# The gated layer's first state: 32x32 transposes on VectorE and a block exchange through DRAM, in place of TensorE transposes

## Chip, cores, metric

One core of one Trainium2 chip. The metric is the device time of one launch in microseconds (us), median over runs. All runs in this document were of the fast state. Runs sent together share one chip and the runs of the kernel before on it; other groups of runs were on other chips, so across groups I compare ratios to the kernel before.

## The reference, cut to what matters

Three graph-attention layers are followed by a gated graph layer, over 128 graphs of 128 nodes and 256 features, all f32:

```python
# --- layer 3 (adj_preln) ---
h = jnp.maximum(_layernorm(x, axis=-1), 0.0)     # the gated layer's first state
x = x + _L3_gnn_ref(h, adj, ...)

def _L3_gnn_ref(x, adj, weight, w_ih, w_hh, b_ih, b_hh):
    h = x
    for i in range(3):
        m = jnp.einsum('bnd,de->bne', h, weight[i])
        aggr = jnp.einsum('bst,bsd->btd', A, m)
        h = _gru_cell(aggr, h, w_ih, w_hh, b_ih, b_hh)
    return h
```

## The kernel before

Graphs go in 32 groups of four (T = 4 x 128 = 512 columns). `gat(g)` does the attention layers and ends with the normalised first state; `gru(g)` does three gated steps. The state is needed twice: node-major as `hn` (for the aggregation) and feature-major as `hT` (for the gates).

```python
def turned(v, pool, tag, name):                       # used in all four layers
    hT = pool.tile([P, KD, T], FT, tag=tag, name=f"hT_{name}")
    for k in range(KD):
        ps = bank("gat", f"hTp_{name}_{k}")
        for b in range(G):
            nc.tensor.transpose(ps[:, b * P : (b + 1) * P], v[:, b, k * P : (k + 1) * P], ident)
        if k % 2 == 0:
            nc.scalar.copy(hT[:, k, :], ps)
        else:
            nc.vector.tensor_copy(hT[:, k, :], ps)
    return hT

# the tail of gat(g)
nm, rs = stats(xt, f"{g}_3")
nc.vector.tensor_mul(nm, nm, rs)
hn = grp.tile([P, G, D], FT, tag="hn0", name=f"hn_{g}_0")
for b in range(G):
    nc.scalar.activation(hn[:, b, :], xt[:, b, :], AF.Relu, bias=nm[:, b : b + 1], scale=rs[:, b : b + 1])
hT = turned(hn, grp, "h0", f"{g}_3")
# ... cut ...

# gru(g), one step: matmuls named nn, r, z read the state h; r, ni, z read the aggregate ag
def evac(k):                                          # steps 1 and 2: node-major state
    if i > 0:
        ps = node_major(i, k)                         # hnp: TensorE transposes into the one "tr" bank
        t = rw.tile([P, G, P], FT, tag=f"hn{k}", name=f"hn_{name}_{k}")
        nc.scalar.copy(t.rearrange("p b d -> p (b d)"), ps)
# ... cut ...
def aggregate(k):                                     # agp: into the same "tr" bank
    ps = bank("tr", f"agp_{name}_{k}")
    for b in range(G):
        nc.tensor.matmul(ps[:, b * P : (b + 1) * P], hn[k][b], am[:, b, :], start=True, stop=True)
    t = rw.tile([P, T], FT, tag=f"ag{k}", name=f"ag_{name}_{k}")
    nc.vector.tensor_copy(t, ps)
    ag.append(t)
# ... cut ...
AHEAD = 2
for g in range(min(AHEAD, NG)):
    run(gat(g))
for g in range(NG):
    run(gru(g))
    if g + AHEAD < NG:
        run(gat(g + AHEAD))
```

The program is emitted in that order, and a scheduler gives each engine a fixed order from it ahead of time (in the trace the 344 matmuls of a turn come in one order for 20 turns). The engines run their orders in parallel (the busy shares of 97%, 57% and 42% below overlap in one span). In the trace the attention of one group runs beside the gated steps of the group before it.

## Time and profile before

| | before |
|---|---|
| time, median | 3158.55 us |
| busy: TensorE / VectorE / ScalarE | 97% / 57% / 42% |
| one turn of a group in the steady part | 95.53 us, 30 of them nearly alike |
| TensorE transposes of the first state | 256 of 128x128, 8 a group |
| output stores: first at | 214.26 us |

In a row of the groups by line or of the timeline, PE is TensorE's matmuls, PEld its weight loads, DVE VectorE, ACT ScalarE. The names are output<-inputs. Brackets or the last column give the idle time just before, and what ended it. For example, in the waits of PE:

```profile
PE hnp L312 <- DVE ag L342: 37.5, 30, 1.5
```

This says that TensorE stood idle 37.5 us in 30 places, once a group and 1.5 us at the longest, before the node-major transposes, until DVE had copied the aggregate out of the bank that both share. A bank is one of the PSUM tiles (`bank(...)` in the code) that TensorE writes its results to.

### The profile page before, as it was taken

To read this page: it belongs to the slowest core of one execution; us is meant where nothing else is said; L and a number is where in the kernel's file an instruction comes from. 1 tells how busy PE (TensorE), PEld (TensorE's weight loads), DVE (VectorE), ACT (ScalarE), POOL (GpSimd) and SP (SyncE) were. 2 spreads that over 40 slices of the span, in tenths; PEclk is the share of its full clock that TensorE was granted. 3 is DMA by queue.
4 is the path that set the end of the run, shared out by engine and by line. 5 is a ranking of instruction groups with operands and counts; after the bars stand their busy time and mean duration, and the time that the engine had idled before them with its cause. 6 is when DMAs were issued, how large, how long until landed. Compare 5 with 4: busy or idle time off the path is not lost.

```text
span 3155.9 us, 31261 instructions
## 1 busy us (share of the span) xinstructions
PE 3049.1 (97%) x11093; PEld 1730.8 (55%) x11093; DVE 1785.9 (57%) x3960; ACT 1316.4 (42%) x2881; POOL 262.3 (8%) x358
## 2 busy tenths in 40 slices
PE   5799999999999999999999999999999999999999
PEld 3455555555555555555555555555555555555554
DVE  4555565555655555655555655556555555555553
ACT  1344444444444444444444444444444444444442
POOL 0110100010101001100001100101000001010000
PEclk8899999999999999999999999999999999999999
DMA  2000000000000000000000000000000000000000
GB/s 84 11 17 17 11 7 17 17 17 13 15 7 17 17 17 10 14 11 17 17 17 11 7 17 17 17 17 10 7 17 17 17 11 17 7 14 7 7 1 14
DMA packets 56188, 47.94 MB, mean 15 GB/s; under 512 B 3296, under 2 KB 55648, under 8 KB 56032
## 3 DMA queue, kind: packets, MB, share of 16 engines
q1 hardware_dynamic: 56032, 45.95, 4.6%
q8 instruction: 87, 1.43, 0.2%
q14 instruction: 69, 0.57, 0.1%
HBM read 29.17 MB, written 16.78 MB: 15 GB/s over the span
## 4 chain that ended last, share of the span: by engine, by line
PE 79%; DVE 11%; ACT 6%; issue 3%; DMA 1%; POOL 0%; SPq 0%; ACTq 0%; DVEq 0%; POOLq 0%
PE r L321 18%; PE z L321 16%; PE whp L207 10%; PE nn L321 9%; PE ni L321 8%; PE agp L338 4%; PE hTp L183 4%; PE hp L256 4%; DVE st L167 3%; DVE u L264 3%; DVE xo L268 2%; PE hnp L312 2%; PE atp L248 2%; ACT pe L232 2%; PE e L216 1%
## 5 line engine op out<-in xcount | busy, mean ns | idle before, releaser
L321 PE MATMUL r<-ag,wc 128*128 128x512 f32 x768 | 381.3, 597 | 0.0
L321 PE MATMUL ni<-ag,wc 128*128 128x512 f32 x768 | 371.3, 592 | 0.0
L321 PE MATMUL z<-ag,wc 128*128 128x512 f32 x768 | 366.0, 592 | 0.0
L207 PE MATMUL whp<-w,hT 128*128 128x258 f32 x1536 | 361.5, 385 | 0.7 <-ACT hT L187 0.7
L207 PEld LDWEIGHTS whp<-w,hT 128*128 128x128 f32 x1536 | 286.8, 191 | 90.5 <-ACT hT L187 39.1
L222 DVE SCALAR_TENSOR_TENSOR em<-e,wh,cap 128x128 f32<-128x128 f32 x384 | 108.1, 344 | 397.3 <-PE e L216 397.3
L367 ACT ACTIVATE r<-r,brz 128x512 f32<-128x512 f32 x192 | 131.9, 687 | 457.5 <-PE r L321 457.5
L211 ACT ACTIVATE wh<-whp,rs 128x258 f32<-128x258 f32 x384 | 183.0, 477 | 264.9 <-PE whp L207 264.7
L369 DVE SCALAR_TENSOR_TENSOR n<-r,wn 128x512 f32<-128x512 f32 x192 | 130.7, 681 | 263.5 <-ACT r L367 263.5
L362 ACT ACTIVATE wn<-nn,bh 128x512 f32<-128x512 f32 x192 | 131.3, 684 | 326.4 <-PE nn L321 326.4
L321 PE MATMUL nn<-h,whh 128*128 128x512 f32 x512 | 264.8, 599 | 0.0
L321 PE MATMUL z<-h,whh 128*128 128x512 f32 x512 | 263.2, 595 | 0.1
L321 PE MATMUL r<-h,whh 128*128 128x512 f32 x512 | 261.6, 592 | 0.0
L338 PEld LDWEIGHTS agp<-am,hn 128*128 128x128 f32 x1536 | 203.3, 193 | 64.4 <-issue 47.6
L321 PEld LDWEIGHTS z<-ag,wc 128*128 128x128 f32 x768 | 143.5, 190 | 168.0 <-issue 167.9
L374 ACT ACTIVATE n<-n,bi 128x512 f32<-128x512 f32 x192 | 137.8, 718 | 233.6 <-DVE n L373 233.6
L244 POOL TENSOR_SCALAR xm<-xo 128x1024 f32<-128x1024 f32 x64 | 66.9, 1045 | 1965.4 <-DVE xo L268 1965.4
L321 PEld LDWEIGHTS ni<-ag,wc 128*128 128x128 f32 x768 | 140.8, 190 | 153.0 <-issue 153.0
L262 ACT ACTIVATE t<-hp 128x512 f32<-128x512 f32 x192 | 114.6, 597 | 263.4 <-PE hp L256 263.3
L264 DVE SCALAR_TENSOR_TENSOR u<-hp,xm 128x512 f32<-128x512 f32 x192 | 132.0, 688 | 149.8 <-ACT t L262 149.8
L338 PE MATMUL agp<-am,hn 128*128 128x128 f32 x1536 | 208.0, 275 | 0.0
L342 DVE COPY ag<-agp 128x512 f32<-128x512 f32 x192 | 130.9, 682 | 124.2 <-PE agp L338 124.2
(84 smaller groups left out, 4400.4 us busy)
## 6 DMA issues: line engine op xcount, KB each, us to landing
x<-in_x_dram SPq DMA_DIRECT2D x32, 512.0 KB, 3.9
out_dram<-o SPq DMA_DIRECT2D x32, 512.0 KB, 2.9
adj<-in_adj_dram SPq DMA_DIRECT2D x32, 256.0 KB, 2.8
w<-in_L_gnn_W_dram SPq DMA_DIRECT2D x3, 256.0 KB, 6.4
ab<-in_L_gnn_a_dram SPq DMA_DIRECT2D x3, 256.0 KB, 6.2
whh_ld<-in_L_gnn_w_hh_dram SPq DMA_DIRECT2D x1, 768.0 KB, 8.2
wih_ld<-in_L_gnn_w_ih_dram SPq DMA_DIRECT2D x1, 768.0 KB, 6.1
gt_ld<-in_L_gnn_weight_dram SPq DMA_DIRECT2D x3, 256.0 KB, 3.6
```

Source lines behind the costliest of these rows:

```text
L183: nc.tensor.transpose(ps[:, b * P : (b + 1) * P], v[:, b, k * P : (k + 1) * P], ident)
L207: nc.tensor.matmul(ps[:, :E], hT[:, k, c * P : (c + 1) * P], W[l][:, k, :], start=(k == 0), stop=(k == KD - 1),)
L211: nc.scalar.activation(wh[:, c, :], ps[:, :E], AF.Copy, scale=rs[:, c : c + 1])
L256: nc.tensor.matmul(hp[:, b * D : (b + 1) * D], at[:, c * P : (c + 1) * P], wh[:, c, :D], start=True, stop=True,)
L264: nc.vector.scalar_tensor_tensor(u, hp, 0.0, xm[:, 2 * j : 2 * j + 2, :].rearrange("p b d -> p (b d)"), op0=OP.max, op1=OP.add,)
L321: nc.tensor.matmul(ps, w[:, k, c * P : (c + 1) * P], v[k], start=start, stop=stop)
L338: nc.tensor.matmul(ps[:, b * P : (b + 1) * P], hn[k][b], am[:, b, :], start=True, stop=True)
L342: nc.vector.tensor_copy(t, ps)
L362: nc.scalar.activation(wn, nn, AF.Identity, bias=bh[:, cn : cn + 1])
L367: nc.scalar.activation(r, pr, AF.Tanh, bias=brz[:, cr : cr + 1], scale=0.5)
L369: nc.vector.scalar_tensor_tensor(n, r, 1.0, wn, op0=OP.add, op1=OP.mult)
L374: nc.scalar.activation(n, n, AF.Tanh, bias=bi[:, cn : cn + 1])
```

## The change

The intent is to take 256 transposes off the busiest engine. VectorE transposes 32x32 blocks (in the trace of after, 64 instructions of 128x512 at 0.69 us) in place of TensorE's 128x128, and one write to DRAM with four reads puts the blocks where a full transpose has them. The five further runs that use this exchange gave the right result; no_transpose, which leaves the block transposes out, is off by a relative error of 0.18. The state then lies in runs of 32 columns, so the matmuls and the subtraction of step 0 read it through a pattern of three dimensions.

```diff
-        hT = turned(hn, grp, "h0", f"{g}_3")
+        tr = gw.tile([P, Q, KD, G, 32], FT, tag="hT", name=f"tr_{g}_3")
+        for k in range(KD):
+            nc.vector.transpose(
+                tr[:, :, k].rearrange("p j b c -> p b j c"),
+                hn[:, :, k * P : (k + 1) * P].rearrange("p b (j r) -> p b j r", j=Q),
+            )
+        d = dram.tile([Q, 32, Q, KD * G * 32], FT, tag="d", name=f"d_{g}")
+        nc.sync.dma_start(
+            d.rearrange("q r j f -> (q r) j f"), tr.rearrange("p j k b c -> p j (k b c)")
+        )
+        hT = grp.tile([P, Q, KD, G, 32], FT, tag="h0", name=f"h_{g}_0")
+        for j in range(Q):
+            nc.sync.dma_start(
+                hT[j * 32 : (j + 1) * 32].rearrange("p q k b c -> p q (k b c)"),
+                d[:, :, j, :].rearrange("q r f -> r q f"),
+            )
 # ... cut ...
-        h = [h0[:, k, :] for k in range(KD)]
+        h = [h0[:, :, k].rearrange("p q b c -> p b q c") for k in range(KD)]
 # ... cut: like(t, v) gives the other operand the same dimensions ...
-                    ps, w[:, k, c * P : (c + 1) * P], v[k], start=start, stop=stop
+                    like(ps, v[k]), w[:, k, c * P : (c + 1) * P], v[k], start=start, stop=stop
-                nc.vector.tensor_sub(d, h[c], n)
+                nc.vector.tensor_sub(like(d, h[c]), h[c], like(n, h[c]))
```

More of the change, by code (lines that the diff above doesn't have):

```diff
@@ L62 @@
     BANKS = {"gat": 3, "gru": 4, "tr": 1}
+    Q = P // 32
     def bank(tag, name):
@@ L158 @@
     setup.close()
+    dram = ctx.enter_context(tc.tile_pool(name="dram", bufs=2, space=bass.MemoryType.DRAM))
     rw = ctx.enter_context(tc.tile_pool(name="rw", bufs=2))
@@ L315, in node_major, with like @@
             return ps
+        def like(t, v):
+            return t.rearrange("p (b q c) -> p b q c", b=G, q=Q) if len(v.shape) == 4 else t
         for i in range(STEPS):
```

## The prediction

> **What bounds the kernel now.** I read the page first: its busy shares, its tenths by slice, and the groups by line.
>
> ```profile
> PE 3049.1 (97%) x11093; PEld 1730.8 (55%) x11093; DVE 1785.9 (57%) x3960; ACT 1316.4 (42%) x2881; POOL 262.3 (8%) x358
> PE   5799999999999999999999999999999999999999
> ```
>
> PE is busy in every slice but the first two, while DVE and ACT are near half. That alone would say that any PE work taken away comes off the time. The modelled ends of matmuls flatter PE, though, so I checked by starts. In the timeline two matmuls of 128x512 start every 0.86 us (0.43 us each, so some 0.107 us for 128 columns). Adding this over one turn of a group (start of one "hTp<-hn" batch to the next, 376.88 to 472.41 us) gives about 90.5 us of streaming in 95.53 us. The steady kernel repeats itself every 95.5 us, some 95% of it PE, the rest small gaps. The largest single gap is the 1.2 us at which the node-major transpose waits for the DVE copy of the aggregate (37.5 us over 30 times in the table of waits).
>
> Then the work that the change takes out, in the groups by line (line, engine, operation, out<-in, count, busy us and mean ns, idle before):
>
> ```profile
> L183 PE MATMUL hTp<-ident,hn 128*128 128x128 f32 x256 | 46.5, 286 | 11.9 <-ACT hn L294 7.6
> L187 ACT COPY hT<-hTp 128x512 f32<-128x512 f32 x128 | 74.9, 585 | 50.3 <-PE hTp L183 46.7
> L189 DVE COPY hT<-hTp 128x512 f32<-128x512 f32 x128 | 88.1, 688 | 104.3 <-PE hTp L183 104.3
> ```
>
> The first row is the disputed transposes alone: 256, that is 8 for each of 32 groups. The two copies serve all four layers, so a quarter (32 each) goes. What one group's batch costs is read in the timeline of PE in the steady part:
>
> ```profile
> 376.02 1.02 PE L321 MATMUL nn<-h,whh 128*128 128x512 f32 x2
> 376.88 0.96 PE L183 MATMUL hTp<-ident,hn 128*128 128x128 f32 x4
> 377.68 1.02 PE L321 MATMUL r<-h,whh 128*128 128x512 f32 x2
> 378.54 0.60 PE L183 MATMUL hTp<-ident,hn 128*128 128x128 f32 x4
> 378.98 1.02 PE L321 MATMUL z<-h,whh 128*128 128x512 f32 x2
> 379.84 1.05 PE L338 MATMUL agp<-am,hn 128*128 128x128 f32 x8
> ```
>
> By starts, the first four take 0.80 us (377.68 - 376.88; 0.37 us over streaming, as each waits for an ACT slice of hn) and the other four 0.44. One group: 1.24 us. The same pattern stands in groups 2 to 31.
>
> [...]The new moving operand of the step-0 matmuls comes in runs of 32 f32[...]; the trace of before has no such operand.
>
> **The change part by part**, for one group.
> PE loses 8 transposes: up to 1.24 us. ACT loses one copy of 0.585 us, DVE one of 0.688.
> DVE gains two transposes of 128x512. The tensor_tensor rows of that size take 0.684 to 0.692 us; I estimate 0.69 each, 1.38 for two. DVE net +0.69 us a group, 22 us in all: 57% busy becomes 58%, no bound.
> DMA: 512 KB written (the output's 512 KB landed in 2.9 us) and four reads of 128 KB (256 KB of adj landed in 2.8 us), with an issue of 0.37 us each on SP: an estimated 2 x 0.37 + 2.9 + 3 x 0.37 + 2.8 = 7.6 us, 9 with the DVE part. 32 MB more on queues that are 5% busy is nothing.
> Is that hidden? hn is complete at 378.2 us, and the first matmul on hT starts at 401.74: slack of 23 us, two and a half times what is needed. In steady groups, hidden. For group 0 it isn't: transposes at 112.49, first use at 115.92. There hn is ready at 113.9, h0 would come at about 123, 7 us later. PE has the next group's attention to do meanwhile, and saves 2 us of transposes; I charge +3 us. Group 1, where the transposes cost some 2.5 us (188.04 to 189.79, with a wait of 1.03), gives that back.
> Step-0 matmuls and the subtraction read the same elements in another order: 0.
>
> Does the 1.24 us come off? This is where I hesitate. What follows needs ACT and DVE, and both are dense just there:
>
> ```profile
> 376.15 2.08 ACT L294 ACTIVATE hn<-xo,nm,rs 128x256 f32<-128x256 f32 x4
> 378.13 0.67 ACT L379 ACTIVATE z<-z,brz 128x512 f32<-128x512 f32 x1
> 378.70 0.57 ACT L329 COPY hn<-hnp 128x512 f32<-128x512 f32 x1
> 379.17 0.58 ACT L187 COPY hT<-hTp 128x512 f32<-128x512 f32 x1
> ```
>
> The aggregate matmuls (agp, at 379.84) need the ACT copy that ends at 379.27, and that copy stands behind the four slices of hn. Without the transposes PE would be done with z at 378.98 + 0.86 - 1.24 = 378.60 and would wait for ACT until about 379.5 (end of the copy, plus some 0.2 us to the matmul, as now from copy to weight load and on). With this order of ACT the gain is 379.84 - 379.5 = 0.34 us, not 1.24. And the DVE copy that frees the single "tr" bank runs thus:
>
> ```profile
> 378.83 0.69 DVE L383 SCALAR_TENSOR_TENSOR d<-z,d 128x512 f32<-128x512 f32 x1 [0.51 <-ACT z L379]
> 379.44 0.68 DVE L189 COPY hT<-hTp 128x512 f32<-128x512 f32 x1
> 380.04 0.68 DVE L385 SCALAR_TENSOR_TENSOR h<-d,n 128x512 f32<-128x512 f32 x1
> 380.93 0.69 DVE L342 COPY ag<-agp 128x512 f32<-128x512 f32 x1 [0.21 <-PE agp L338]
> ```
>
> One DVE transpose fits nearly into the idle 0.51 us, the second takes the place of the copy. If both stand ahead of the ag copy, it starts at about 381.1 instead of the 380.6 that an earlier agp would allow, and the gain is gone.
>
> **The rivals**, for 30 steady groups, with start-up +0.5 (3 - 2.5).
> A: PE alone bounds, and the scheduler rearranges ACT so that nothing waits: 30 x 1.24 = 37 us, 3121. For it: 97% busy PE, near-zero gaps in the 20 us around. Against: the order of ACT above.
> B: the wait for hn transposed becomes a wait for the node-major copy on ACT: 30 x 0.34 = 10 us, 3148. For it: the timeline above, where that copy is 0.57 us ahead of its use.
> C: DVE delays the aggregate's copy by the second transpose: gain 0 to -0.1 us a group, 3158 to 3162. For it: DVE is 4.34 us busy of the 5.5 from 376.5 to 382.
> D: the step-0 matmuls (768, 24 a group) slow down on the runs of 32. A tenth more would be 768 x 0.043 = 33 us, and eat all of A.[...]
> E: the exchange isn't hidden and PE waits at each group's start: excluded by the slack of 23 us unless the transfers take three times my estimate.
> The instructions are ordered by a static scheduler, since attention of one group and recurrence of another are mingled in the trace though emitted apart. Removing instructions can shift that order everywhere, by some us either way; nothing in the profile sizes this.
>
> **Range and chances.** Weights: A 0.35, B 0.4, C 0.2, D or E 0.05 (taken at 3190). 0.35 x 3121 + 0.4 x 3148 + 0.2 x 3160 + 0.05 x 3190 = 3143; as schedules between A and B are likely when ACT loses a copy too, I move it to 3140, a gain of 0.6%. The range runs from just under A (3118) to the time before (3158). 2% is 63 us: more than all PE time of these transposes, so faster by 2% needs a lucky new order (0.02); slower by 2% needs D in force, or E (0.03).
>
> **What would show it.** Right: PE matmuls down by 256 and no "hTp<-hn" row; 64 DVE transposes near 0.69 us; step-0 matmuls still starting 0.43 us apart; the first matmul of a group on h0 not waiting for DMA, except in group 0; a turn of 94.3 us (A), 95.2 (B) or 95.5 (C) in place of 95.53. B shows as agp waiting for the ACT copy of hn, C as a longer wait of hnp for ag than 1.2 us a group. Wrong: DVE transposes well above 1 us, step-0 matmuls further apart, a DMA wait in front of nn, or a turn whose order of streams is altogether different.

## The result, and the profile after

The changed kernel takes 3143.81 us (3142.61 to 3145.15, 4 runs) against 3158.55. The ratio is 0.9952, with a 95% interval of 0.9935 to 0.9970. Ratios are the mean time of one kernel's fast runs over that of the other's in the same rounds, so not quite the ratio of the medians. The verdict by the 2% rule is "same", with a small gain clear of noise.

The page's busy line, and the row of the new operation in the groups by line:

```profile
PE 3017.8 (96%) x10837; PEld 1709.2 (54%) x10837; DVE 1803.2 (57%) x3992; ACT 1298.0 (41%) x2849; POOL 263.1 (8%) x358
L302 DVE STREAM_TRANSPOSE tr<-hn 128x512 f32<-128x512 f32 x64 | 41.7, 690 | 3.2 <-ACT hn L296 3.2
```

There are 256 matmuls fewer, and 64 block transposes of 0.69 us each (two in a row take 1.30). PE is still busy 96% of a shorter span. The same stretch of TensorE that the prediction showed now reads, in the timeline of PE:

```profile
380.25 1.02 PE L343 MATMUL nn<-h,whh 128*128 128x512 f32 x2
381.12 1.02 PE L343 MATMUL r<-h,whh 128*128 128x512 f32 x2
381.97 1.02 PE L343 MATMUL z<-h,whh 128*128 128x512 f32 x2
383.56 1.16 PE L360 MATMUL agp<-am,hn 128*128 128x128 f32 x8 [0.56 <-ACT hn L351]
384.55 0.82 PE L185 MATMUL hTp<-ident,xn 128*128 128x128 f32 x6
385.21 1.07 PE L343 MATMUL nn<-h,whh 128*128 128x512 f32 x2
386.11 0.60 PE L330 MATMUL hnp<-ident,h 128*128 128x128 f32 x4
```

The transposes are gone from between nn, r and z, and a wait stands where they were. The aggregate's matmuls come 1.59 us after the start of z, where z's streaming takes 0.86. The bracket names what TensorE waited for: the ACT copy of the node-major state. ACT at that time:

```profile
380.39 2.08 ACT L296 ACTIVATE hn<-xo,nm,rs 128x256 f32<-128x256 f32 x4
382.37 0.67 ACT L401 ACTIVATE z<-z,brz 128x512 f32<-128x512 f32 x1
382.94 0.57 ACT L351 COPY hn<-hnp 128x512 f32<-128x512 f32 x1
```

The order of ACT is the one of before, with the copy behind the four slices of hn; only the copy for hT behind it is gone. It ends at 383.51 and agp starts at 383.56. In the waits of PE over the whole run a row has appeared that wasn't there before:

```profile
PE agp L360 <- ACT hn L351: 16.9, 30, 0.6
```

To see the whole turn and not one place, I took every matmul's start from the trace, averaged over 20 steady groups. I called "streaming" the columns at 0.429 us for 512 (the median spacing within an unbroken run; the 258 columns of whp count as 256), and put the rest down as gaps in front of the instruction that came late. This ledger is my own sum from the traces, in us for one turn:

| | turn | streaming | gaps | before hTp<-hn | before agp | before hnp | before r<-ag |
|---|---|---|---|---|---|---|---|
| before | 95.58 | 90.95 | 4.64 | 0.39 | 0.22 | 1.51 | 0.22 |
| after | 94.91 | 90.09 | 4.82 | none | 1.06 | 1.51 | 0.41 |

The change takes 0.86 of streaming and 0.39 of gaps out, 1.25 in all, as the prediction sized it. Of that, 0.83 comes back before agp and 0.19 before r<-ag. Small gaps elsewhere fall by 0.45 together. The 0.19 is partly a trade with them: at one of the places where r<-ag now waits, the kernel before has a gap of 0.10 before a transpose of the attention (atp). The net is 0.67 us a turn, some 20 us over 30 turns. The first output store leaves at 219.16 us in place of 214.26, so the start costs 4.9 us. 20 less 5 is the 15 us measured.

### The profile page after: what moved, and what is told of

Read it like the earlier page. It is cut to its first block, busy times and chain, and to the rows that moved or that the text cites. A ratio compares the mean times of both kernels' runs of the same rounds, so it can differ in the third digit from the quotient of the medians.

```text
span 3141.2 us, 31050 instructions
## 1 busy us (share of the span) xinstructions
PE 3017.8 (96%) x10837; PEld 1709.2 (54%) x10837; DVE 1803.2 (57%) x3992; ACT 1298.0 (41%) x2849; POOL 263.1 (8%) x358
## 4 chain that ended last, share of the span: by engine, by line
PE 77%; DVE 11%; ACT 7%; issue 3%; DMA 1%; POOL 0%; SPq 0%; DVEq 0%; POOLq 0%; ACTq 0%
PE r L343 17%; PE z L343 15%; PE whp L209 11%; PE nn L343 9%; PE ni L343 8%; PE agp L360 5%; PE hp L258 4%; PE hTp L185 3%; DVE st L169 3%; DVE u L266 3%; DVE xo L270 2%; PE hnp L330 2%; ACT pe L234 2%; ACT hn L296 2%; PE atp L250 2%
## 5 line engine op out<-in xcount | busy, mean ns | idle before, releaser
L343 PE MATMUL nn<-h,whh 128*128 128x512 f32 x768 | 394.2, 595 | 1.6 <-DMA h<-d 1.2
L343 PE MATMUL r<-h,whh 128*128 128x512 f32 x768 | 393.2, 594 | 0.0
L343 PE MATMUL z<-h,whh 128*128 128x512 f32 x768 | 392.4, 592 | 0.0
L360 PE MATMUL agp<-am,hn 128*128 128x128 f32 x1536 | 212.9, 278 | 23.1 <-ACT hn L351 16.9
L343 PEld LDWEIGHTS r<-h,whh 128*128 128x128 f32 x768 | 141.0, 191 | 139.8 <-issue 117.2
```

Of the source, the lines that this page charges most:

```text
L343: nc.tensor.matmul(like(ps, v[k]), w[:, k, c * P : (c + 1) * P], v[k], start=start, stop=stop)
```

## The experiments

My theory at this point was that the ACT copy holds back what the transposes free (rival B of the prediction), against rival C, that DVE does. Nine kernels were run; each row is of one kernel and the last column its ratio to the kernel before.

| run | time, us | turn, us | ratio |
|---|---|---|---|
| after_tail_late | 3144.25 | 94.93 | 0.9951 |
| before_tail_late | 3142.58 | 95.05 | 0.9947 |
| after_hn_pool | 3342.11 | 101.29 | 1.0579 |
| no_transpose | 3150.44 | 95.12 | 0.9970 |
| after_tail_late_tr_behind | 3125.41 | 94.33 | 0.9891 |
| first_on_pe | 3140.79 | 94.93 | 0.9940 |
| best1 | 3122.86 | 94.38 | 0.9883 |
| layout_only | 3159.50 | 95.60 | 1.0000 |
| before_plus_exchange | 3157.13 | 95.49 | 0.9994 |

### after_tail_late and before_tail_late: only the order of ACT

The tail of `gat` is emitted inside the gated steps of the group before, behind its step-2 copies, so that the copy gets ahead of three of the four hn slices. The same edit is made to both kernels.

```diff
     for g in range(NG):
-        run(gru(g))
+        step = gru(g)
+        if g + 1 in tails:
+            advance(step, 13)          # past step 2's node-major copies and aggregates
+            run(tails.pop(g + 1))
+        run(step)
         if g + AHEAD < NG:
-            run(gat(g + AHEAD))
+            tails[g + AHEAD] = gat(g + AHEAD)
+            advance(tails[g + AHEAD], 12)   # all but the tail
```

> The changed kernel with one thing moved: the last part of a group's attention (statistics, scaled relu to hn, exchange) is emitted inside the recurrence of the group before, after its step-2 node-major copies, so that ACT does the node-major copy ahead of three of the four hn slices. Same instructions otherwise. Theory (the saved 1.24 us of PE turned into a wait of the aggregate for that ACT copy): the wait of agp for ACT hn, 16.9 us over 30 groups in the changed kernel, falls below 3 us, the turn of a group falls from 94.89 us to 94.3 to 94.5, the time to 3125 to 3133. Rival C (DVE's two transposes ahead of the ag copy bound): turn and time stay, 94.9 and 3144.

> The same move in the kernel before, as the control: is it the order alone that gains? Theory: with the transposes in place PE had only about 0.35 us to gain from an earlier copy, as PE reached agp just then, so a turn between 95.2 and 95.6 and 3148 to 3160. Rival (the new order alone gives the gain, whatever becomes of the transposes): a fall as large as between the changed kernel and its moved form, about 15 us, to 3143.

The theory failed in both, and in both the number of its rival came out. The wait for ACT did vanish, as wanted (gaps before agp 0.31 in place of 1.06), but the changed kernel stayed at 3144.25 us. The kernel before gained all of it: 3142.58, ratio 0.9947. With this order the change is worth nothing. PE and DVE of after_tail_late tell where the time went, in the timelines of the two engines:

```profile
385.01 1.05 PE L360 MATMUL agp<-am,hn 128*128 128x128 f32 x8
385.90 1.12 PE L343 MATMUL nn<-h,whh 128*128 128x512 f32 x2
386.86 1.02 PE L343 MATMUL r<-h,whh 128*128 128x512 f32 x2
388.25 0.66 PE L330 MATMUL hnp<-ident,h 128*128 128x128 f32 x4 [0.37 <-DVE ag L364]
```

```profile
385.76 0.16 DVE L172 TENSOR_SCALAR nm<-mv 128x4 f32<-128x4 f32 x1
386.32 1.30 DVE L302 STREAM_TRANSPOSE tr<-hn 128x512 f32<-128x512 f32 x2 [0.39 <-ACT hn L296]
387.55 0.65 DVE L364 COPY ag<-agp 128x512 f32<-128x512 f32 x1
390.78 0.69 DVE L364 COPY ag<-agp 128x512 f32<-128x512 f32 x1 [2.58 <-PE agp L360]
```

Now the hn slices come later, the two transposes wait for them at the head of DVE's order (0.39 us), and the copy of the aggregate stands behind. It starts at 387.55, 1.65 us after the aggregate's last matmul gave way to nn (385.90). TensorE needs that copy for the bank. The gap of the ledger before hnp grew from 1.51 to 2.09. So C stands behind B: take the wait for ACT away in this way and the wait for DVE takes its place. The edit has a part in that, as it delays three of the four hn slices that the DVE transposes need. The table of waits shows the second as hnp waiting 60 times (48.4 us) where the changed kernel waited 30.

The kernel before has no DVE transposes, so it can use the early copy. Its eight TensorE transposes now run as one batch once hn is complete, as the timeline of PE shows:

```profile
382.40 1.07 PE L338 MATMUL agp<-am,hn 128*128 128x128 f32 x8
383.31 1.04 PE L183 MATMUL hTp<-ident,hn 128*128 128x128 f32 x8
384.18 1.88 PE L321 MATMUL r<-ag,wc 128*128 128x512 f32 x4
```

The gap before them fell from 0.39 to 0.02, that before r<-ag from 0.22 to 0.03.

### after_tail_late_tr_behind: both waits out of the way

Kept from after_tail_late: the late tail. New: the DVE transposes are queued behind the first copy of the aggregate, where DVE was idle for 2.58 us.

```diff
+                cp = nc.vector.tensor_copy(t, ps)
+                if i == STEPS - 1 and k == 0:
+                    last_ag[g] = cp.ins
 # ...
+            with ExitStack() as behind:
+                if g - 1 in last_ag:
+                    behind.enter_context(tc.issue_after(last_ag[g - 1]))   # order only
+                nc.vector.transpose(...)
```

> The first run's theory fell as told: with the ACT copy early the wait for ACT is gone, but the turn stayed at 94.9 us, and the same move gained the kernel before 16 us. New theory: two waits lie one behind the other at this place. The changed kernel waits 0.73 us a group for the ACT copy; with that gone it waits for DVE, whose two transposes stand ahead of the copy of the aggregate (gaps of 0.54 us before hnp and 0.2 us within r<-ag). This run keeps the late tail and also queues the DVE transposes behind that copy, where DVE idled 2.6 us. Theory: the 0.54 and 0.2 go, turn 94.1 to 94.3, time 3118 to 3128. Rival (PE's streaming is not the floor here, something else of this schedule holds 94.9): turn and time stay within 0.1 us and 4 us of 94.93 and 3144.

It took 3125.41 us, ratio 0.9891, turn 94.33, as expected of the theory save 0.03 us on the turn. DVE's order is now the wanted one:

```profile
384.32 0.69 DVE L368 COPY ag<-agp 128x512 f32<-128x512 f32 x1 [0.17 <-PE agp L364]
384.93 1.29 DVE L306 STREAM_TRANSPOSE tr<-hn 128x512 f32<-128x512 f32 x2
388.39 0.69 DVE L368 COPY ag<-agp 128x512 f32<-128x512 f32 x1 [2.17 <-PE agp L364]
```

The gap before hnp fell from 2.09 to 1.54; that before r<-ag stayed at some 0.22, so the second part of the expectation (0.2 us there) was a miss. Against before_tail_late, the kernel that keeps its TensorE transposes in the same late order, the change is now worth 95.05 - 94.33 = 0.72 us a turn and, by the ratios, 0.56%. This pair shows most of the 0.86 of streaming arriving at last.

### no_transpose and before_plus_exchange: what the added parts cost

no_transpose (a wrong result on purpose) writes hn to DRAM as it is and reads it back by the same transfers.

```diff
-        tr = gw.tile(...)
-        for k in range(KD):
-            nc.vector.transpose(...)
# ... cut ...
-            d.rearrange("q r j f -> (q r) j f"), tr.rearrange("p j k b c -> p j (k b c)")
+            d.rearrange("q r j f -> (q r) j f"), hn.rearrange("p b (j f) -> p (b j) f", j=1)
```

> Wrong result on purpose: the changed kernel without its two DVE transposes, hn written to DRAM as it is and read back by the same five transfers. Tells what the DVE part costs. Theory (ACT copy bounds, DVE's 1.3 us lies beside it): turn 94.7 to 94.9, time 3139 to 3144. Rival C (the DVE part delays the aggregate's copy): turn down by 0.3 us or more, 3135 or less.

It took 3150.44 us, more than the changed kernel although it does less, so neither number held. The wait for the ACT copy is unchanged (gap of 0.73 us between z and agp in both). So is the gap before hnp, where a late copy of the aggregate would show (some 1.52 us a turn in both). With DVE's transposes absent neither the time nor these gaps fell, so in the changed kernel as it stands they are not what holds TensorE at this place. The 0.2 us a turn that this kernel loses comes with another static order: behind agp stands one attention transpose, where the changed kernel has six (the row at 384.55). The ledger finds nothing of the loss there. It lies in small gaps before matmuls of the attention (0.12 to 0.13 us more before each of hTp<-xn, atp and whp), less 0.19 before r<-ag. What makes them is not isolated.

before_plus_exchange adds the two DVE transposes, the write and the four reads to the kernel before, into a tile that nobody reads.

```diff
         hT = turned(hn, grp, "h0", f"{g}_3")
+        tr = ...; nc.vector.transpose(...)   # as in the change
+        d = ...;  hx = grp.tile(..., tag="hx", bufs=1)   # five transfers into hx
```

> The added parts alone: the kernel before still transposes on TensorE and uses that state; beside it each group also does the two DVE transposes, the write and the four reads into a tile that nobody reads. Theory (DVE's part stands ahead of the copy of the aggregate and has some 0.5 us too little room): the copy moves from 5.35 to about 5.9 us after the first nn of the step, the turn grows by 0.3 to 0.7 us, the time to 3168 to 3182. Rival (the added parts are hidden and cost nothing by themselves): 3156 to 3163.

It took 3157.13 us, ratio 0.9994 (0.9985 to 1.0003): the added parts cost nothing by themselves, as the rival said, and my theory was a miss. Its 5.35 us counts from the start of the node-major transposes (375.58 to 380.93), not from the first nn; by that count the copy now starts at 5.80. Again the order bent around them, as its timeline of PE shows:

```profile
382.00 1.05 PE L357 MATMUL agp<-am,hn 128*128 128x128 f32 x8
382.89 1.01 PE L186 MATMUL hTp<-ident,xn 128*128 128x128 f32 x6
383.74 1.07 PE L340 MATMUL nn<-h,whh 128*128 128x512 f32 x2
```

The copy is later, but six transposes of the next attention stand between agp and nn and TensorE works on them meanwhile. My theory had kept the old order of PE.

### after_hn_pool: hn on GpSimd

```diff
-            nc.scalar.activation(hn[:, b, :], xt[:, b, :], AF.Relu, bias=nm[...], scale=rs[...])
+            nc.gpsimd.tensor_scalar(hn[:, b, :], xt[:, b, :], rs[...], nm[...], op0=OP.mult, op1=OP.add)
+        nc.gpsimd.tensor_scalar(hn, hn, 0.0, None, op0=OP.max)
```

> The changed kernel with hn (the four scaled relu slices) computed on GpSimd in place of ACT, so ACT is free for the node-major copy. Theory: agp no longer waits for ACT, turn 94.3 to 94.6, time 3126 to 3135. Rival C (DVE): stays at 3144. A second way to be wrong: GpSimd is slower on these and hn comes late, which costs nothing as the exchange has over 10 us of slack.

It took 3342.11 us, 5.8% more than before. ACT was free, and hn came late, which I had thought harmless. The timeline shows why it isn't:

```profile
392.63 3.16 POOL L296 TENSOR_SCALAR hn<-xo,rs,nm 128x256 f32<-128x256 f32 x4 [0.38 <-PE hnp L331]
395.88 2.78 POOL L299 TENSOR_SCALAR hn<-hn 128x1024 f32<-128x1024 f32 x1
398.69 1.30 DVE L303 STREAM_TRANSPOSE tr<-hn 128x512 f32<-128x512 f32 x2 [3.86 <-POOL hn L299]
399.92 0.65 DVE L408 SCALAR_TENSOR_TENSOR h<-d,n 128x512 f32<-128x512 f32 x1
400.62 2.08 PE L344 MATMUL nn<-h,whh 128*128 128x512 f32 x2 [4.64 <-DVE h L408]
```

hn takes 6 us here instead of 2.1. The DVE transposes wait 3.86 us for it, and what stands behind them on DVE waits too, though it doesn't need hn. The new state h is ready to go when its last input d is done at 394.83 (d<-z,d: 394.15, 0.68 us), but it starts at 399.92, behind the two transposes, 5.09 us later. The copy of the aggregate, whose matmuls start at 394.93, follows at 400.77. TensorE idles 4.64 us for h (139.3 us in 30 waits). The exchange had its slack; DVE's place in the order had none. The idle time is 4.64 of the 6.4 us that a turn grew. Behind it the granted clock, the share of its full clock at which the profile shows TensorE, is 0.50 (400.6 to 403 us), and the two nn matmuls take 2.08 us where they took 1.02; over the whole run the granted clock is 0.965, in the other runs 0.99. As a test of the ACT theory this run is confounded: agp no longer waits for ACT, but the turn says nothing for or against the theory.

### first_on_pe: the start

```diff
+        if g < 1:
+            hT = turned(hn, grp, "h0", f"{g}_3")
+        else:
             # the exchange
```

> The changed kernel with the first group's state alone transposed on TensorE as before. Theory: the first output store left 4.9 us later than before (219.16 against 214.26 us), as the exchange of group 0 is not hidden and the static order left PE waiting 3.4 us behind it; with it undone the first store is back within 1 us of 214, and the time falls by 4 to 6 us to 3138 to 3140, the turn unchanged at 94.9. Rival (the start is lost to something else): store and time unchanged.

It took 3140.79 us, ratio 0.9940 against 0.9952, turn unchanged. The first store is at 216.19 us, so 3.0 of the 4.9 us came back, not all. The direction was right and the size short by two fifths. (The intervals of the two ratios overlap, so it is the store that shows the gain, not the ratio.) In the changed kernel the first nn of group 0 waits 1.15 us for the exchange, and worse, the static order has a transpose of the next attention next, as its timeline shows:

```profile
122.83 1.10 PE L343 MATMUL nn<-h,whh 128*128 128x512 f32 x2 [1.15 <-DMA h<-d]
127.31 1.09 PE L250 MATMUL atp<-ident,pe 128*128 128x128 f32 x4 [3.38 <-DVE pe L241]
```

TensorE idles for DVE's pe while the r and z matmuls, which read the same h as nn, stand behind atp (r starts at 128.19).

The record shows two things behind the part that did not come back. The granted clock is 0.50 from 116 to 119 us in first_on_pe, where the kernel before already has 1.00. At the node-major transposes of group 0's last step it is 2.28 us behind that kernel (185.67 against 183.39), of which 0.74 was there when the first state was transposed (113.23 against 112.49). Then TensorE waits 1.89 us for the DVE copy of an aggregate (before ni, at 191.62), in the stretch where the changed kernel wins time back from group 1. Why the clock comes up later is not shown.

### layout_only: the operand in runs of 32

```diff
+            cp(hT[:, :, k].rearrange("p q b c -> p b q c"),      # blocked tile, written from PSUM
+               ps.rearrange("p (b q c) -> p b q c", b=G, q=Q))
```

with the readers of step 0 as in the change.

> The kernel before with only the new layout: states still transposed on TensorE, the two copies write the blocked tile, and step 0 reads it through the 32-element runs. Tells what the operand costs by itself. Theory: nothing, step-0 matmuls 429 ns apart, 3155 to 3162. Rival D: a tenth slower, some 33 us more.

It took 3159.50 us, ratio 1.0000 (0.9991 to 1.0008). The spacing of matmuls that read runs of 32 has a median of 429 to 430 ns in both kernels that do (after and layout_only), and 429 to 430 for contiguous reads. In these runs the layout costs nothing.

### best1: the three together

Late tail, transposes behind the copy, first group on TensorE.

> Candidate: late tail, transposes behind the copy, first group on TensorE. Theory: both gains add, turn 94.1 to 94.3 and the first store near 215: 3113 to 3123. Rival: as the single runs say, no less than the lower of them.

It took 3122.86 us (3122.37 to 3123.52), ratio 0.9883: 0.7% below the changed kernel by the ratios, and the best here. The turn is 94.38 and the first store at 216.11 us; both miss the expected turn and store slightly.

## Why the prediction was right, point by point

- **The time.** 3143.8 us was measured, 3140 predicted, within the range. The gain was 0.48% by ratio, forecast 0.6%. That the centre lies so near is in part luck. 3140 is a weighted mean of the rivals, moved by hand, and no mechanism's own sum: B's was 3148. B had 0.34 us a turn where 0.67 was measured, some 10 us too little gain, and the start was 4.4 us too cheap, the other way.
- **1.24 us a group as the size of what is removed.** Right: 0.86 streaming and 0.39 gaps, 1.25.
- **B, the wait for the ACT copy.** Seen as told, in a row that the page of before doesn't have (16.9 us over 30). Its size was off. I charged 0.23 us from the end of the copy to agp; it was 0.05 (383.51 to 383.56). From the start of the node-major transposes to agp it is 3.74 us after and 4.26 before, so 0.52 us gained at this place where I had 0.34. The rest up to 0.67 is spread over small gaps in a new order, and no run isolates it. The turn of 94.91 lies between A (94.3) and B (95.2).
- **C, DVE.** Not what holds the changed kernel itself (no_transpose), but after_tail_late shows it behind B, with an edit that itself delays the DVE transposes. That B and C would stack was not in the prediction: it weighed them as alternatives. Breaking B alone brings nothing, breaking both brings the rest.
- **D and E.** D is excluded by layout_only (ratio 1.0000). That it was unlikely was my estimate; no trace of before showed it. E was rightly ruled out for steady groups: the transposes start at 382.50 us and the reads are issued from 386.58 with a median of 3.8 us to landing, so the state is there at about 392, against a first use at 405.46.
- **The start.** Mis-sized: +0.5 us predicted as the net of the first two groups, 4.9 measured. The wrong term is group 0's +3 us: at the node-major transposes of its last step, before group 1's state comes in, the changed kernel is 6.99 us behind (190.38 against 183.39). h0 came at the time told (nn starts at 122.83, told about 123), but the next attention did not fill the time: TensorE waits 1.15 us for h0 and 3.38 us for pe. From 125 to 131 us, within and behind the second wait, the granted clock is 0.50, where the kernel before has 1.00, and the r matmul at 128.19 lasts 1.06 us against a median of 0.59; by my estimate the 4 us of work from 127.3 on lose some 2 us to that. Group 1 did give back what was told, 2.36 us of 2.5: at the next r<-ag the changed kernel is 4.63 us behind (198.33 against 193.70).
- **DVE's cost and the scheduler.** 0.69 us an instruction, as told; DVE's busy time grew by 17.3 us, told 22. That the order "can shift everywhere" was told and not sized; before_tail_late shows that order alone is worth as much as the whole change, 0.53% by the ratios.

Still open: why the small gaps of no_transpose grew, why the granted clock comes up later at the start of first_on_pe, and the gap of some 1.4 us between a z and an hnp that all these kernels share, where TensorE waits for the copy of the aggregate. To remove that was not tried, nor were the DVE transposes queued behind the copy without the late tail, which would tell what C is worth alone.

## What to carry to other kernels

Work taken off a 97% busy engine came off the time here only up to the next instruction there that depends on another engine (of 1.25 us a turn, 0.83 came back before agp); look at what that engine does just ahead of it, and then at what stands behind that wait. Where a scheduler fixes the order ahead of time, try the new order on the old kernel too: here that control gained as much as the change. What an added instruction cost here was its place in the order of its engine: the same two transposes cost 0.60 us a turn more in after_tail_late than in after_tail_late_tr_behind. So put it where that engine idles (here behind the copy of the aggregate), not where its input is first ready.

## Other figures from these runs

- Transposes of f32 on VectorE: 0.69 us for 128x512 (median 691 ns) and 1.30 us for two in a row, which start 0.635 us apart (median of 32 pairs in after).
- Transposes of f32 on TensorE: each of 128x128 lasts a median of 273 ns, but eight in one batch take 0.87 us by starts (before_tail_late), some 0.11 us each. The duration taken alone would overstate the cost by two and a half times.
- Matmul operands in runs of 32 f32: 429 to 430 ns for 512 columns, as contiguous.
- tensor_scalar on GpSimd: a spread of 2.7 on one shape, 128x1024 f32 with one tensor input. A multiply and add with immediates took 1.05 us, a max with one immediate, in place, 2.78. No run isolates what makes the difference. With two per-partition scalars, 128x256 took 0.56 us (median).
